# Four attention heads' maxima taken ahead, maxima rows on another queue, keys before queries

## The chip, the core and the metric

One core of one Trainium2 chip runs the whole kernel. The metric is the device time in microseconds (us) of one execution; the median of three runs before the change is 1075.11 us.

## The reference

The input is 2 sequences of 1024 tokens with 128 values each, all f32. Four blocks follow each other, each added to its input and followed by a layer norm:

```python
x = _layernorm(x + _L0_attn_ref(x, ...))   # retention, 8 heads
x = _layernorm(x + _L0_ffn_ref(x, ...))    # causal attention, then experts
x = _layernorm(x + _L1_attn_ref(x, ...))   # full attention
x = _layernorm(x + _L1_ffn_ref(x, ...))    # 128 x 128 matrix, ternary weights
```

The retention has scores `q @ k.T` with a decay by distance and no softmax, then a group norm for each head, a gate (`silu`) and an output matrix. Both attentions have 16 heads of width 8. Each head's row of scores goes through a softmax: exponentials of the scores less the row's maximum, divided by their sum. The first attention is causal; after it each token goes to the one of 4 experts (hidden width 512) that its logits favour. The second attention has biases in queries, keys and values, and two corner scores set to -1e9.

## The kernel before

The work of the two sequences is laid out as two long stages, with TensorE (PE) as the engine that has most to do.

*The retention* runs from the start to about 241 us. It goes through 16 chunks of 128 tokens, one per turn of a loop. A turn n has, in the engines' order: the scores of chunk n; `gated` and `affine` (group norm's scale, bias and gate) of chunk n-1, with VectorE's product `og * sg` (L1018 in the last turn); `weighted` (scores times values, from `sm`), the running state (`carry`, `state`, L858 and L861), `group_norm(n)` (its sum of squares is `ss`, L868, its `rstd` comes from GpSimd, L139 and L140) and `normal` (ScalarE's `on`, L879), and `output(n-1)` with the Wo matrix, residual and the statistics of the layer norm. The PSUM tiles of the stage come from pools of their own; `rwide` gives a tile of two banks. Jobs that make the queries and keys of the first attention for early tokens are placed into turns by a table `plan` and a function `aside`.

*The chain* runs from about 241 us to the end, and covers both attentions. A step (a, b, k, g, h) is attention a, sequence b, key half k of 512 keys (so also which half of the tokens), a group g of 4 heads, and a block h of 256 queries. Each step has three parts, spread over "ticks" of the function `chain_tick`:

- In its s-items, TensorE writes up to 512 scores for each of the 4 heads of the group (`score`, tile `sc`, a bank of PSUM each), and VectorE takes the maxima of each row (`maxima`): L430 with a plain reduction, L425 where the diagonal has to be masked. The result is a column in `parts`.
- After a step's last s-item, `shifts` (L437) joins the parts and negates them (`lowered`). In the next tick `product` has TensorE transpose that (`turn`, L444, into a free corner of the bank `acc`), and `enter` has ScalarE copy it to `m_rows` (L450) and a DMA write it into additional rows of `qT`, from row ONE of each head on (L452, 4 KB, 64 times, on SyncE's queue). These rows are summed into the next scores by the matmul itself, so they come out less the maximum.
- Seven ticks after an s-item (AHEAD = 7), `shifted` has TensorE compute the scores once more, transposed (`sct`: 256 keys by 256 queries of a head in one bank), `exps` has ScalarE take the exponentials of them (L485, tile `es`, four for each tick), `bar` has GpSimd zero the part above the diagonal (L493), and one tick later `product` multiplies by the values into `acc`. ScalarE copies `acc` out (L518 for a first pair of keys, L521 for the others, which GpSimd then adds, L522). Two ticks later `finish` transposes and divides.

One tick of the later kind thus has four `sc`, four `sct` and one `acc`: nine allocations, each the next bank of a ring of the eight PSUM banks (`ring_of`). In chain_tick the heads are taken as (0, 1) and (2, 3): scores of two, shifted scores of two, then the others. The order of the instructions on each engine is written by hand here (`manual_schedule`): an engine takes them strictly in that order. `side_work(tick)` runs before each tick and advances lanes of jobs: generators in which a `yield n` says how many ticks later the next piece may be emitted. There are 208 ticks of items.

Between the two stages stands a stretch written out by hand: ticks 0 to 4 of the chain, among them what the last turn of the retention still has to do: `output(14)`, `normal(15)`, `gated(15)` and `affine(15)` (L907 and L909: og times scale plus bias), the product `og * sg` of chunk 15 (L1044; L1043 ahead of it is an exponential of one value whose result isn't used), `output(15)` (its statistics are L924 to L927), `aside(15, 1)`, and `layer_norm_scalar` (rstd on GpSimd by L139 and L140, shift on GpSimd by L932 and L933, then the norm itself on ScalarE, L935). Ticks 5 and on follow in a loop.

The jobs that the change touches: the experts' lane gathers a sequence's tokens ordered by expert (`e_in`, L1256, a DMA on SyncE), yields 2 ticks (L1257), and transposes them (`xg_ps`, L1265); its weights come by L1236 (`e_w`, SyncE). `attn_inputs` makes values, queries and keys of the second attention for half a sequence; its last loop (L1387) computes `dense` for the queries and then for the keys (ScalarE's bias add, L1393), and `spread` (L280) writes each into `qT` or `kT` with four DMAs on SyncE's queue, one for each head group.

Of the kernel before, what the change touches and what calls it, by code (L numbers as in the profile page):

```python
# [18 lines left out]
NC = BT // P  # L19
QT = 2  # L20
BQ = QT * P
RH, RD, RV = 8, 64, 128
NG, GH, HD = 4, 4, 8
HW = 32
# [40 lines left out]
def block_kernel(  # L65
# [13 lines left out]
    nc = tc.nc  # L79
# [101 lines left out]
    def slot(name):  # L181
        return banks[0](name)
# [213 lines left out]
                if n < len(p):  # L396
                    mm(*p[n])

    def score(item, heads):
        i, pieces = item  # L400
        a, b, k, g, h = steps[i]
        if i not in parts:
            parts[i] = small.tile([P, QT, GH, NB], F32, tag="parts", name="parts")
        got = []
        for j in heads:
            sc = slot("sc")
            rws = hrows(j)
            products = []
            for c, first, n, at, _ in pieces:
                tok = (queries(i) * QT + c) * P  # L410
                products.append((
                    sc[:, at : at + n], qT[b][rws, g, tok : tok + P], kT[b][rws, g, first : first + n]
                ))
            got.append((j, sc, products))
        return got
# [30 lines left out]
    def enter(i, tp):  # L446

        a, b, k, g, h = steps[i]
        rows_of = small.tile([GH * QT, P], F32, tag="m_rows", name="m_rows", bufs=2)
        nc.scalar.copy(rows_of, tp[: GH * QT])  # L450
        at = queries(i) * BQ
        nc.sync.dma_start(out=qT[b][ONE::HW, g, at : at + BQ], in_=rows_of)  # L452

    def diagonal_pair(n_item):
        i, pair = t_items[n_item]
# [109 lines left out]
    def starts(a, b, k):  # L565
        return s_first[step_of(a, b, k, 0, 0)]

    def chain_tick(tick):
        si = tick if tick < n_items else None
        ti = tick - AHEAD if 0 <= tick - AHEAD < n_items else None  # L570


        for s_heads, t_heads in (((0, 1), (2, 3)), ((2, 3), (0, 1))):
            got_s = got_t = ()
            for second in (s_heads[0] > 0, s_heads[0] == 0):
                if second and ti is not None:
                    got_t = shifted(ti, t_heads)
                elif not second and si is not None:
                    got_s = score(s_items[si], s_heads)
            together(*(products for *_, products in (*got_s, *got_t)))  # L580
            if si is not None:
                maxima(s_items[si], got_s)
            if ti is not None:
                exps(ti, got_t)
        if ti is not None:
            bar(ti)
        if si is not None and s_last[s_items[si][0]] == si:
            shifts(s_items[si][0])
        si, entering = tick - 1, None
        if 0 <= si < n_items and s_last[s_items[si][0]] == si:  # L590
            entering = s_items[si][0]
        ai = tick - AHEAD - 1
        if 0 <= ai < n_items:
            product(ai, entering)
        elif entering is not None:
            tp = slot("m_ps")[:, :P]
            turn(entering, tp)
            enter(entering, tp)
        ai = tick - AHEAD - 3
        if 0 <= ai < n_items and t_last[t_items[ai][0]] == ai:  # L600
            finish(t_items[ai][0])


    with ExitStack() as rc:
# [233 lines left out]
        def weighted(n, sm):  # L838
            for g in range(RG):
                for a in range(2):  # L840
                    nc.tensor.matmul(  # L841
                        pout[n][:, a, g, :], sm[:, a, g, :], v[n][:, 2 * g + a, :],
                        start=opens(n) and g == 0, stop=True, skip_group_check=True,
                    )
# [95 lines left out]
        def layer_norm(m, r):  # L940
            for c in range(NC):
# [2 lines left out]
                    ALU.subtract, ALU.mult,  # L944
                )


        plan = {
            (3, 1): (pad, 1), (4, 0): (pad, 1), (4, 1): (pad, 1), (5, 0): (pad, 3),
# [15 lines left out]
        with tc.manual_schedule():  # L965
            for n in range(3):
                transpose_x(n)
            pr = rotary(0)
            center()
            cosines(0, pr)  # L970
            cosines(1, rotary(1))
            values(0)
            gate(0)
            sines(0)
            rotated(0)
            late_loads = load_late()
            next(late_loads)
            block = None
            for n in range(n_chunks - 1):
                before = n > 0  # L980
                keeps = not opens(n + 1)
                sm = scores(n)
                if keeps:
                    kd = keys_by_token(n)
                sines(n + 1)
                rotated(n + 1)
                if before:
                    pt, og = gated(n - 1)
                    affine(n - 1, pt, og, range(RH))
                weighted(n, sm)  # L990
                if keeps:
                    carry(n, kd)
                if before:
                    nc.vector.tensor_tensor(og, og, sg[n - 1], ALU.mult)  # L994
                r = group_norm(n)
                if n + 2 < n_chunks:
                    cosines(n + 2, rotary(n + 2))
                next(late_loads, None)
                gate(n + 1)
                if block:  # L1000
                    layer_norm(*block)
                    block = None
                aside(n, 0)
                normal(n, r)
                if before:
                    block = output(n - 1, og)
                values(n + 1)
                aside(n, 1)
                if n + 3 < n_chunks:
                    transpose_x(n + 3)  # L1010
                if n == 2:
                    dense_weights()
            n = n_chunks - 1
            sm = scores(n)
            pt, og = gated(n - 1)
            affine(n - 1, pt, og, range(RG), range(RG, RH))
            weighted(n, sm)
            nc.vector.tensor_tensor(og, og, sg[n - 1], ALU.mult)  # L1018
            r = group_norm(n)
            aside(n, 0)  # L1020
# [7 lines left out]
        ))  # L1028
        banks[0] = ring_of(ring)
        with tc.manual_schedule():  # L1030
            chain_tick(0)
            output(n - 1, og)
            normal(n, r)
            rs.close()
            ring.append(ctx.enter_context(tc.tile_pool(
                name="ring2", bufs=1, space=PSUM, side="right", reuse_waits="tile"
            )))
            chain_tick(1)
            pt, og = gated(n)
            affine(n, pt, og, range(RH))  # L1040

            unused = small.tile([P, 1], F32, tag="unused", name="unused")
            nc.scalar.activation(unused, col("one"), AF.Exp)  # L1043
            nc.vector.tensor_tensor(og, og, sg[n], ALU.mult)  # L1044
            chain_tick(2)
            chain_tick(3)
            block = output(n, og)
            chain_tick(4)
            alone.clear()
            aside(n, 1)  # L1050
            layer_norm_scalar(*block)
# [161 lines left out]
    def experts(oh, endings_of, quick=False):  # L1213
# [40 lines left out]
        bias_1 = found["bias_1"]  # L1254
        rows_in = scratch("e_rows", "e_in", (P, NT, P))
        nc.sync.dma_start(out=rows_in[:, :n_tiles], in_=by_e)  # L1256
        yield 2  # L1257
        xgT = scratch("e_cols", "xgT", (P, NT, P))
        for at in range(0, n_tiles, NC):
            if at and n > NC:  # L1260
# [102 lines left out]
    def attn_inputs(b, k):  # L1363

        at, name = ((0, "k_first"), (T - 1, "k_last"))[k]
        t = kT[b][:, :, at]
        nc.gpsimd.tensor_tensor(t, t, col(name).to_broadcast([P, NG]), ALU.add)
        if k == 0:

            for g in range(NG):  # L1370
                nc.sync.dma_start(
                    out=qT[b][ONE::HW, g, :],
                    in_=causal[:GH, :P].unsqueeze(1).to_broadcast([GH, T // P, P]),
                )
        tp = transposed(x2[b][k], "x2_ps")
        x2T = scratch("joT", "x2T", (P, BT))
        nc.scalar.copy(x2T, tp)
        yield 1
        pv = by_tile(x2T, lw["wv"], "lpv")
        for c in range(NC):  # L1380
            nc.vector.tensor_tensor(
                v_heads(b)[:, k * NC + c, :, :HD],
                pv[:, c * P : (c + 1) * P].rearrange("p (h d) -> p h d", d=HD),
                row("bv").rearrange("p (h d) -> p h d", d=HD),
                ALU.add,
            )
        for dst, w, name, tag in (  # L1387
            (qT[b], lw["wq"], "bq", "sq"), (kT[b], lw["wk"], "bk", "xn")
        ):
            pr = slot("lpr")  # L1390
            mm(pr, w, x2T)
            dense = scratch(tag, "dense", (P, BT))
            nc.scalar.activation(dense, pr, AF.Identity, bias=bias[name])  # L1393
            spread(dst, k, dense)
        yield 1
# [116 lines left out]
                    lane.pop(0)  # L1512

    with tc.manual_schedule():
        for tick in range(5, last_tick):
            side_work(tick)
            chain_tick(tick)
        side_work(last_tick)
# [132 lines left out]
```

## Time and profile before

| what | before |
|---|---|
| median of 3 runs | 1075.11 us (1066.61 to 1077.7) |
| the profiled execution | 1074.85 us |
| its span, first to last instruction | 1073.2 us |
| mean granted TensorE clock | 0.972 |
| the retention | 0 to about 241 us |
| from the retention to the tick with the first product | about 241 to 283 us |
| exponentials L485 on ScalarE | 418.4 us, 832 of 587 ns |
| maxima L430 on VectorE | 397.6 us, 640 of 682 ns |
| maxima L425 on VectorE | 125.6 us, 256 of 491 ns |
| matmuls `sc`, `sct`, `acc` on TensorE | 423.1, 409.4 and 220.4 us |
| DMA issues of `qT<-m_rows` (L452) | 64 of 4.0 KB, on SyncE's queue |

All but the first two lines of the table come from one execution, recorded by the profiler. PE is TensorE's matmuls, PEld its weight loads (which overlap the matmuls), DVE is VectorE, ACT ScalarE, POOL GpSimd, SP SyncE; SPq is SyncE's queue of DMA issues. In a group's row `out<-in` are the names of the tiles, `xcount` is the number of instructions, and after the bar stand busy time, mean duration in ns, and the idle time of the engine just before these instructions with what ended most of it. In the strip of 40 slices each digit is the busy share in tenths, and a slice is 26.8 us; PEclk is the clock that TensorE was granted, in tenths of its full speed. A row of an engine's order of time has start and duration in us, then engine, line and operation; square brackets hold the idle time before it and what ended that.

### The profile page before, as it was taken

Reading aid. Unit: us, or ns where it says so; the run is one execution under the profiler, and the core shown is the slowest. Engines: PE = TensorE matmul, PEld = TensorE weight load, DVE = VectorE, ACT = ScalarE, POOL = GpSimd, SP = SyncE. Lnnn points to the kernel's source line nnn. Section 1 sums busy time; section 2 is a strip of 40 time slices with the busy share of each in tenths; the row PEclk is TensorE's granted clock in tenths of the full one; section 3 lists DMA queues with packets and bytes.
Section 4 is the critical chain, followed back from the end, with each engine's and each line's share of the span. In section 5 each row is a group of like instructions: output and inputs, shape, how many; then the busy total and the mean of one; then the engine's idle time right before and its main releaser. Section 6 shows DMA issues by size and latency. Waiting matters only on the chain.

```text
span 1073.2 us, 28623 instructions
## 1 busy us (share of the span) xinstructions
PE 1012.6 (94%) x11455; PEld 721.6 (67%) x11455; DVE 768.7 (72%) x1747; ACT 685.8 (64%) x1482; POOL 458.4 (43%) x626
## 2 busy tenths in 40 slices
PE   6999999997899999989999999999999999999995
PEld 5888888875565657765776666677756666666662
DVE  4667686667774867777677787766686888888861
ACT  2555544544575767665767677766676777777774
POOL 2466554533354664465444334425271222222222
PEclk9999999998897999999999999999999999999997
DMA  6522122110100032103311000323102000000000
GB/s 207 141 63 50 40 49 48 24 31 2 39 2 17 6 82 87 39 14 84 93 38 23 3 2 7 102 61 100 29 24 41 2 13 2 13 2 3 11 3 10
DMA packets 31061, 43.10 MB, mean 40 GB/s; under 512 B 4496, under 2 KB 18000, under 8 KB 30800
## 3 DMA queue, kind: packets, MB, share of 16 engines
q1 hardware_dynamic: 29664, 38.89, 14.0%
q0 software_dynamic: 1024, 2.10, 0.7%
q8 instruction: 90, 1.47, 0.6%
q10 hardware_dynamic: 240, 0.29, 0.1%
q14 instruction: 43, 0.35, 0.1%
HBM read 23.83 MB, written 4.46 MB: 26 GB/s over the span
## 4 chain that ended last, share of the span: by engine, by line
PE 74%; DVE 11%; POOL 5%; DMA 4%; issue 2%; ACT 2%; SPq 1%; POOLq 0%; DVEq 0%; ACTq 0%
PE sc L86 17%; PE acc L86 16%; PE sct L86 14%; DVE spare L425 3%; PE ph L86 2%; PE pmoe L86 2%; PE pout L841 2%; PE py L86 2%; PE pr L86 2%; PE pv L86 2%; DVE parts L430 2%; PE o_ps L211 1%; PE mpr L86 1%; PE pg L86 1%; PE psc L86 1%
## 5 line engine op out<-in xcount | busy, mean ns | idle before, releaser
L485 ACT ACTIVATE es<-sct 128x512 f32<-128x512 f32 (+1 forms) x832 | 418.4, 587 | 171.5 <-PE sct L86 150.1
L430 DVE TENSOR_REDUCE parts<-sc 128x1 f32<-128x512 f32 x640 | 397.6, 682 | 105.1 <-PE sct L86 90.1
L86 PE MATMUL sc<-kT,qT 32*128 32x512 f32 (+3 forms) x1792 | 423.1, 585 | 8.7 <-DVE parts L425 5.0
L86 PE MATMUL sct<-qT,kT 32*128 32x256 f32 (+1 forms) x3328 | 409.4, 389 | 3.9 <-DMA qT<-m_rows 3.9
L86 PEld LDWEIGHTS sct<-qT,kT 32*128 32x128 f32 x3328 | 292.5, 187 | 23.7 <-issue 7.9
L522 POOL TENSOR_TENSOR oT<-oT,part 128x256 f32<-128x256 f32 x144 | 104.6, 727 | 331.9 <-ACT part L521 331.4
L86 PE MATMUL acc<-es,v_aug 128*32 128x256 f32 (+1 forms) x3328 | 220.4, 382 | 10.5 <-DVE parts L430 4.2
L86 PEld LDWEIGHTS sc<-kT,qT 32*128 32x128 f32 x1792 | 154.6, 189 | 78.8 <-issue 25.9
L86 PEld LDWEIGHTS acc<-es,v_aug 128*32 128x32 f32 x3328 | 89.7, 111 | 105.8 <-DVE parts L430 40.5
L425 DVE CUSTOM_DVE_ANT_0 spare<-sc,causal 128x128 f32<-128x128 f32 (+3 forms) x256 | 125.6, 491 | 45.0 <-PE sct L86 11.6
L909 ACT ACTIVATE og<-pt,cols_sb 128x128 f32<-128x128 f32 x124 | 45.0, 467 | 43.3 <-PE pt L896 43.3
L493 POOL TENSOR_SCALAR_AFFINE_SELECT es<-es 128x512 f32<-128x512 f32 x64 | 40.3, 635 | 62.7 <-ACT es L485 60.9
L521 ACT COPY part<-acc 128x256 f32<-128x256 f32 x144 | 56.9, 395 | 7.7 <-PE acc L86 6.1
L140 POOL TENSOR_TENSOR rstd<-rstd,nhalf 128x4 f32<-128x4 f32 (+2 forms) x46 | 55.5, 1208 | 3.7
L778 POOL TENSOR_TENSOR qd<-qk,r_rest 128x512 f32<-128x512 f32 x16 | 20.3, 1271 | 49.1 <-DVE qk L775 46.2
L795 ACT COPY v<-pv 128x1024 f32<-128x1024 f32 x16 | 16.2, 1012 | 38.6 <-PE pv L86 38.6
L772 POOL TENSOR_TENSOR swap<-swap,r_cs 128x1024 f32<-128x1024 f32 x15 | 35.4, 2360 | 10.7 <-DMA swap<-plain 10.7
L86 PE MATMUL py<-r_wo,og 128*128 128x128 f32 x256 | 33.1, 285 | 2.5 <-DVE og L994 2.5
L86 PEld LDWEIGHTS py<-r_wo,og 128*128 128x128 f32 x256 | 31.3, 200 | 3.7 <-PE pg L86 1.1
L86 PE MATMUL pv<-r_wv,xT 128*128 128x512 f32 x64 | 30.6, 601 | 2.2 <-DVE qk L768 2.0
L841 PE MATMUL pout<-v,sm 128*128 128x128 f32 x256 | 31.5, 277 | 1.2 <-DVE sm L809 1.2
L86 PE MATMUL pg<-xT,r_wg 128*128 128x128 f32 x256 | 31.4, 276 | 1.1 <-ACT v L795 1.1
(236 smaller groups left out, 1262.8 us busy)
## 6 DMA issues: line engine op xcount, KB each, us to landing
e_w<-in_m_w SPq DMA_DIRECT2D x50, 256.0 KB
swap<-plain SPq DMA_DIRECT2D x62, 128.0 KB
qT<-dense SPq DMA_DIRECT2D x32, 64.0 KB
kT<-dense SPq DMA_DIRECT2D x32, 64.0 KB
x<-in_x SPq DMA_DIRECT2D x4, 256.0 KB
mcs<-in_m_const SPq DMA_DIRECT2D x4, 256.0 KB
qT<-m_rows SPq DMA_DIRECT2D x64, 4.0 KB
e_in<-by_expert SPq DMA_DIRECT2D x2, 448.0 KB
```

Of the source, the lines that this page charges most:

```text
L86: nc.tensor.matmul(o, lhsT, rhs, start=start, stop=stop)
L140: nc.gpsimd.tensor_tensor(r, r, nhalf[:, :n], ALU.pow)
L425: nc.vector.tensor_tensor_reduce(out=spare[:, :n], in0=sc[:, at : at + n], in1=causal[:, BT - n :], scale=1.0, scalar=-3.0e38, op0=ALU.add ...
L430: nc.vector.tensor_reduce(part, sc[:, at : at + n], AX.X, ALU.max)
L485: nc.scalar.activation(es[n_item][:, j, :n], sct[:, :n], AF.Exp, scale=scale)
L493: nc.gpsimd.affine_select(out=d, in_=d, pattern=[[0, GH], [1, P]], compare_op=ALU.is_ge, fill=0.0, base=0, channel_multiplier=-1,)
L521: nc.scalar.copy(part, acc[:, :BQ])
L522: nc.gpsimd.tensor_tensor(sum_, sum_, part, ALU.add)
L772: engine.tensor_tensor(swap[n], swap[n], table(n, 1), ALU.mult)
L778: nc.gpsimd.tensor_tensor(qd[n], rq[n], gq, ALU.mult)
L841: nc.tensor.matmul(pout[n][:, a, g, :], sm[:, a, g, :], v[n][:, 2 * g + a, :], start=opens(n) and g == 0, stop=True, skip_group_check=True,)
L909: nc.scalar.activation(to, of, AF.Identity, bias=bias_, scale=weight)
```

## The change

It has four parts, in the words of the diff:

- The score banks and maxima of tick 0 (all four heads) and of the first two heads of tick 1 are emitted inside the last two turns of the retention, with a new function `ahead_of_time`, in a pair of banks of the retention's `rwide` instead of the ring. Tick 0 is the only s-item of its step, so `shifts` follows there, after heads 2 and 3. `taken` holds that half of tick 1 is done, and `chain_tick(1)` only does heads 2 and 3. `chain_tick(0)` is gone, and each of the hand-written ticks moves up a place: the stretch starts at tick 1 and ends with tick 5, so `output(15)` now comes after tick 4 and the loop begins with tick 6.
- The DMA of the maxima's row is issued by ScalarE's queue, behind the copy that makes the row.
- The experts' lane of the second sequence waits three ticks instead of two before the transposes of the gathered tokens.
- In `attn_inputs` the keys come ahead of the queries.

```diff
-    def score(item, heads):
+    def score(item, heads, bank=lambda: slot("sc")):
...
-            sc = slot("sc")
+            sc = bank()
...
-        nc.sync.dma_start(out=qT[b][ONE::HW, g, at : at + BQ], in_=rows_of)
+        nc.scalar.dma_start(out=qT[b][ONE::HW, g, at : at + BQ], in_=rows_of)
...
+    taken = set()
...
-                elif not second and si is not None:
+                elif not second and si is not None and not (si in taken and s_heads[0] == 0):
                     got_s = score(s_items[si], s_heads)
...
+        def ahead_of_time(tick, heads):
+
+            wide = rwide("sc")
+            at = iter(range(2))
+            got = score(
+                s_items[tick], heads, lambda: wide[:, next(at)].rearrange("p g t -> p (g t)")
+            )
+            together(*(products for *_, products in got))
+            maxima(s_items[tick], got)
+            if heads[0]:
+                assert s_last[s_items[tick][0]] == tick
+                shifts(s_items[tick][0])
+            else:
+                taken.add(tick)
...
                 weighted(n, sm)
+                if n + 2 == n_chunks:
+                    ahead_of_time(0, (0, 1))
                 if keeps:
                     carry(n, kd)
...
                 aside(n, 0)
+                if n + 2 == n_chunks:
+                    ahead_of_time(0, (2, 3))
                 normal(n, r)
...
             affine(n - 1, pt, og, range(RG), range(RG, RH))
+            ahead_of_time(1, (0, 1))
             weighted(n, sm)
             nc.vector.tensor_tensor(og, og, sg[n - 1], ALU.mult)
             r = group_norm(n)
...
-            chain_tick(0)
+            chain_tick(1)
             output(n - 1, og)
             normal(n, r)
...
-            chain_tick(1)
+            chain_tick(2)
             pt, og = gated(n)
             affine(n, pt, og, range(RH))
...
             nc.vector.tensor_tensor(og, og, sg[n], ALU.mult)
-            chain_tick(2)
             chain_tick(3)
+            chain_tick(4)
             block = output(n, og)
-            chain_tick(4)
+            chain_tick(5)
             alone.clear()
             aside(n, 1)
             layer_norm_scalar(*block)
...
-        yield 2
+        yield 2 if n == NC else 3
...
         for dst, w, name, tag in (
-            (qT[b], lw["wq"], "bq", "sq"), (kT[b], lw["wk"], "bk", "xn")
+            (kT[b], lw["wk"], "bk", "xn"), (qT[b], lw["wq"], "bq", "sq")
         ):
...
-        for tick in range(5, last_tick):
+        for tick in range(6, last_tick):
             side_work(tick)
             chain_tick(tick)
```

## The prediction

> **What bounds the kernel now.** I read the busy shares first, then TensorE's own waits, then the granted clock in short windows around each wait, and last the engines' orders of time where something is moved. The page's first two views:
>
> ```profile
> PE 1012.6 (94%) x11455; PEld 721.6 (67%) x11455; DVE 768.7 (72%) x1747; ACT 685.8 (64%) x1482; POOL 458.4 (43%) x626
> ...
> PEclk9999999998897999999999999999999999999997
> ```
>
> TensorE is the bound nearly everywhere: in the later ticks one full tick takes 2.95 us without a hole (starts at 686.65, 689.59, 692.53). So a gain must come from holes in TensorE's row, or from slices with a lower clock. TensorE's waits (us in total, times, longest) name four such holes, all on DMAs that the change touches, besides the start:
>
> ```profile
> PE sct L86 <- DMA qT<-m_rows: 3.9, 3, 1.8
> ...
> PE xg_ps L1265 <- DMA e_in<-by_expert: 1.8, 1, 1.8
> ...
> PE sc L86 <- DMA kT<-dense: 1.0, 1, 1.0
> ```
>
> (The first row is three waits: 1.85, 1.17 and 0.88 us, ended at 331.4, 397.1 and 506.7.) What such a hole costs is more than itself. Windows of 4 us; the columns are the busy times of PE, PEld, DVE, ACT, POOL, then the granted clock:
>
> ```profile
> 328.00:332.00 4.00, 2.15 (x17) 1.16 (x17) 2.53 (x10) 1.25 (x2) 1.17 (x3) 1.00 0.15 18
> 332.00:336.00 4.00, 4.00 (x39) 2.09 (x35) 1.29 (x2) 2.59 (x6) 0.04 (x1) 0.65 0.01 2
> 336.00:340.00 4.00, 4.00 (x13) 2.76 (x12) 0.00 (x0) 1.17 (x2) 0.68 (x1) 0.50 0.00 1
> 340.00:344.00 4.00, 4.00 (x20) 2.08 (x23) 0.27 (x1) 1.26 (x3) 1.61 (x1) 0.50 0.00 0
> 344.00:348.00 4.00, 4.00 (x36) 2.13 (x28) 2.31 (x4) 2.45 (x5) 3.01 (x3) 0.64 0.06 20
> ```
>
> The reader is to see a window with a hole (2.15 of 4 busy), then 16 us with TensorE full and its clock down: work at half speed.
>
> **The change part by part.** *The rows on ScalarE's queue.* Why was the row at 331.4 late? Its copy (L450) ran at 322.0; then SyncE's queue:
>
> ```profile
> 324.41 2.87 SPq L280 DMA_DIRECT2D qT<-dense  x4
> 327.38 0.56 SPq L452 DMA_DIRECT2D qT<-m_rows  x1
> ```
>
> The row lay 5.1 us behind a wait for `dense` and the four issues of it; it landed 3.9 us after its issue began. The same stands at 388.6 to 393.48 (four kT issues ahead) and at 498.9 to 501.29 (part of eight). Issued by ScalarE right after the copy, they come 5.1, 4.6 and 2.4 us sooner; landing even as slowly as the worst of the three (5.3 us), at 327.6, 394.2 and 504.2, they precede the moments where TensorE ran dry (329.6, 395.9, 505.9). All three holes go.
>
> Their price: hole plus clock. First: 1.85 + 4 x (0.35 + 0.50 + 0.50 + 0.36) = 8.7 us. Second, windows of 3 us from 397 at 0.67 and 0.76: 1.17 + 3 x (0.33 + 0.24) = 2.9. Third, from 507 at 0.55 and 0.89: 0.88 + 3 x (0.45 + 0.11) = 2.6. Sum 14.1 us.
>
> Here two rules of the Trainium skill speak against this. "DMA: Bandwidth & Descriptors", section "Issuing engines are not separate DMA queues", says that DMAs of all issuers share the same 16 engines, and that another issuer saves only the sequencer's time to start one. By that the rows would land no sooner and the 14.1 would stay. The rows above show that the lost time is not in the transfer: 5.1 us passed before the issue, in SyncE's order. I take the rows. "TensorE: Matmul & The Clock Gate", section "HAM oscillation — how this bites in real kernels", warns only of idle gaps over about 3.4 us; by it holes of 0.9 to 1.9 us cost no clock, and the three are worth 3.9 us, not 14.1. The trace shows a fall after each of these three, and after the two priced below; but holes of 1.48 us (664.1) and 1.11 us (798.3) left it at 1.00. So I take the measured falls, and keep the idle time alone as the other end.
>
> Against that stands ScalarE's issue time. The nearest row is its own two DMAs (L758): 593 and 602 ns, begun 0.03 us after the copy; SyncE's 64 row issues took 521 to 630. I take 0.57 us, 64 times: 36.5 us if nothing covers it. Queued behind are the copy of `acc` (L518, L521), which frees a PSUM bank, then the four exponentials of the next tick; TensorE waits for both through its ring of eight banks, GpSimd for the copies (it idles 331 us on them, and nobody waits for it). The cover, in a later tick with a row:
>
> ```profile
> 924.20 0.25 ACT L450 COPY m_rows<-acc 8x128 f32<-8x128 f32 x1
> 924.36 0.36 ACT L518 COPY oT<-acc 128x256 f32<-128x256 f32 x1
> ...
> 925.39 2.06 ACT L485 ACTIVATE es<-sct 128x512 f32<-128x512 f32 x4 [0.68 <-PE sct L86]
> ```
>
> ScalarE then idles 0.68 us: the issue fits with 0.1 to spare, and the bank is free at 925.3, before TensorE's fourth pair at 925.47. So the last 32 steps cost nothing. In the first 32 rows come every one to four ticks and the ticks are shorter; I put 0.1 us on each, 3.2 us, an estimate between 0 and the 18.2 of all 32 uncovered. SyncE is rid of 64 waits; expert weights behind them come sooner, but TensorE waits for none of those.
>
> *Keys ahead of queries (L1387).* At 582.02 the queries' four issues went first (2.90 us), the keys at 585.04, landing at about 590.1, and TensorE stood 1.03 us until 590.16; the clock was then 0.77 and 0.66 in 3 us windows. Keys first land 3 us sooner, before 589.1. The queries of that half are first read 30 ticks later. Gain 1.03 + 3 x (0.23 + 0.34) = 2.7 us.
>
> *`yield 3` (L1257).* `e_in`, issued at 691.07, landed 6.3 us later, 1.77 us after its transposes were due; the clock was 0.80 and 0.77 in the next 4 us windows. One tick (2.95) later it has landed with 1.2 to spare: 1.77 + 4 x (0.20 + 0.23) = 3.5 us. What follows slides a tick, keys of the second sequence too, with five ticks (15 us) in hand: no cost.
>
> *Maxima taken ahead.* Tick 0's eight pairs run from 243.71 to 247.31, 3.6 us of VectorE, 1.8 for two heads; two of 512 take 1.7 (steps of 0.84). 5.3 us leave a stretch that VectorE paces: that is the ceiling. In turn 14 VectorE idles 2.44 us before `state` (for L858) and 2.04 before `on` (for rstd). The first 1.8 starts only after `weighted` (226.64) and its 0.64 us of matmuls, so it ends at 229.1 and delays state, og, ss by 0.6; the second hides. In turn 15 the pair stands between L907 and L1018 with no idle: 1.7 more. So `ss` ends 2.3 us later (246.1), and `on` on ScalarE at 250.2 instead of 248.0. Counting on from 246.1 with the same durations (half tick 1 1.7, output 0.85, tick 2 2.85, about 1.2 waiting for `on`, then waiting for og until 255.3, og 1.2, tick 3 3.6) VectorE finishes tick 3 at 260.1, not 261.85. But the last `output` now follows tick 4 (3.4 us) and ends at 264.3 instead of 262.8. A chain hangs on it:
>
> ```profile
> 262.88 0.20 POOL L139 TENSOR_SCALAR rstd<-mv 128x4 f32<-128x4 f32 x1 [15.94 <-DVE mv L927]
> ...
> 272.01 0.24 POOL L933 TENSOR_SCALAR shift<-shift 128x4 f32<-128x4 f32 x1
> ```
>
> Then L935 on ScalarE (272.28, 1.65 us) stands ahead of the first exponentials. Unchanged in length, it releases them at 275.5 instead of 273.98. VectorE's lead is thus stopped there. Before, these exponentials waited 1.48 us between their halves; now they run through and end at 277.2 as before, and tick 8 starts 0.5 to 0.8 us sooner. I take 0.7 gained, between 1.5 lost (that wait stays) and 5.3 gained (the chain is not the brake). The three row issues that stand there lie in ScalarE's idle time.
>
> Sum: 14.1 + 2.7 + 3.5 + 0.7 - 3.2 = 17.8 us. The profiled execution took 1074.85 us (span 1073.2); 1074.85 - 17.8 = 1057.0. The median of the runs, 1075.11, is 0.3 above that execution, so I predict 1057 us.
>
> **The rivals.** (a) *The clock does not pay.* Holes go, but falls of the clock come elsewhere: two longer holes caused none, so which hole does is partly chance. Only idle time counts: 3.9 + 1.0 + 1.8 + 0.7 - 3.2 = 4.2, 1070.7 us. For it: 8.5 of the 20.3 us come from four windows after a single hole. Against it: five of five DMA holes were followed by a fall.
> (b) *The rows land no sooner*, the change doing nothing for them as the first rule says: 1074.85 - 2.7 - 3.5 - 0.7 + 3.2 = 1071.1. Against it: the 5.1 us.
> (c) *ScalarE becomes the brake.* Each issue is paid in full on the way from `acc` to the next exponentials: 36.5 us lost against 21.0 gained, 1090.3 us, slower. It decides from 37 of the 64 issues (21.0 / 0.57). For it: the margin at 924 is 0.1 us, and a row issue may also have to wait on ScalarE for an expert weight load to land (the row after 397.1, with six loads from 395.87). Against it: ScalarE waits for TensorE before exponentials nearly every tick (150.1 us over 193 times).
> (d) *The start gains its ceiling*: 1057.0 - 4.6 = 1052.4, if L935 does not hold the exponentials. It only widens the main case.
>
> **How the numbers follow.** Main case with (d) 0.60, (a) 0.20, (b) 0.10, (c) 0.10. A measurement of this kernel tells about 1% from no change. Under 1064.4 lies the main case: faster 0.60. (a), (b): within 1%, 0.30. (c): slower, 0.10. The range runs from the ceiling with no ScalarE cost (1052.4 - 3.2 = 1049) to just past (b), 1072, leaving out (c). The likeliest case alone: 1049 to 1064.
>
> **What would show it.** TensorE's waits have no row for `qT<-m_rows`, `kT<-dense`, `e_in`; the clock is 1.00 where 332 to 348 stood; the row issues stand on ScalarE's queue with about 0.57 us and its idle time before L485 falls by some 30 us; in the start, `ss` of turn 15 ends about 2.3 us later, and L935 still comes just ahead of the first exponentials. Wrong would prove me: clock falls in new places with no DMA behind them; new TensorE waits on `es`, `part` or `oT`; exponentials starting well before 275.

## The result and the profile after

The changed kernel takes 1079.71 us (median of 8 runs, 1079.11 to 1080.56) against 1073.1 us for the kernel before (8 runs, 1066.61 to 1077.7). The ratio is 1.0058, with a 95% interval from 1.0035 to 1.0081: some 6 us slower, where 16 to 18 us less were predicted. It lies outside the predicted range (1049 to 1072).

The profiled execution took 1079.37 us, its span is 1077.7 us, and its mean granted clock is 0.982 (before: 0.972). So the clock is better and the time is worse. The execution profiled before was a slow one of its kernel, by its clock, so the changed kernel is compared below with profiles at 0.982 and 0.984 too. The page's shares of busy time and the strip of the granted clock:

```profile
PE 1027.4 (95%) x11455; PEld 725.9 (67%) x11455; DVE 768.3 (71%) x1747; ACT 693.1 (64%) x1482; POOL 459.5 (43%) x626
...
PEclk9999999997899999999999999999999999999997
```

TensorE has the same 11455 matmuls and 14.8 us more busy time, at a higher clock. The three holes of the prediction (on rows, on keys, on `e_in`) are gone: TensorE's list of waits names no DMA in the chain any more. The same five windows that ran at half clock before:

```profile
328.00:332.00 4.00, 4.00 (x52) 2.74 (x45) 3.46 (x15) 3.17 (x8) 2.20 (x4) 1.00 0.18 23
332.00:336.00 4.00, 4.00 (x32) 2.32 (x32) 1.26 (x3) 3.06 (x8) 0.72 (x1) 1.00 0.00 1
336.00:340.00 4.00, 4.00 (x49) 2.88 (x48) 2.49 (x4) 2.92 (x6) 3.05 (x2) 1.00 0.01 4
340.00:344.00 4.00, 4.00 (x54) 2.61 (x53) 2.98 (x8) 2.33 (x5) 1.78 (x3) 1.00 0.21 49
344.00:348.00 4.00, 3.30 (x44) 2.04 (x48) 3.53 (x13) 2.14 (x6) 3.63 (x5) 1.00 0.14 17
```

That much went as written. One fall of the clock came in a new place, though: 3.4 us at half clock from 478.9 on, behind 1.6 us of waiting for VectorE's `parts` and no DMA (TensorE's waits from 470 to 480 us, and a window):

```profile
PE acc L86 <- DVE parts L430: 1.6, 1, 1.6
...
478.00:482.00 4.00, 4.00 (x36) 2.93 (x28) 3.74 (x10) 1.46 (x3) 3.92 (x6) 0.62 0.02 4
```

The loss shows in the page's groups, in the idle time just before ScalarE's two copies out of `acc` (the last part of each row; before, L521 had 7.7 us of it and L518 3.8):

```profile
L521 ACT COPY part<-acc 128x256 f32<-128x256 f32 x144 | 56.1, 389 | 21.5 <-ACT m_rows L450 9.7
...
L518 ACT COPY oT<-acc 128x256 f32<-128x256 f32 x64 | 24.3, 379 | 27.7 <-ACT m_rows L450 22.5
```

Together 32.2 us behind `m_rows` L450: that is where ScalarE issues the DMA, and issuing isn't counted as busy. The wait list of TensorE hardly has it:

```profile
PE sc L86 <- DVE r L1444: 1.1, 1, 1.1
...
PE sc L86 <- ACT part L521: 0.7, 1, 0.7
...
PE sc L86 <- ACT oT L518: 0.7, 1, 0.7
```

So the ticks have to be compared one by one. A tick is taken here from the first `acc` matmul of the tick before it to its own. The price of a row shows plainly in the second attention. Some ticks from both profiles (us):

```
tick  row?   before  after
164           3.73    3.15
165   yes     4.08    3.98
166           2.94    4.08     (a job slid by one tick)
167           2.94    2.94
168           3.16    3.16
169   yes     2.94    3.49
173   yes     2.93    3.50
177   yes     2.93    3.50
181   yes     2.94    3.49
```

By tick 126 the changed kernel is 9.1 us ahead, at the end it is 5 us behind. Clock makes up most of the lead: between 300 and 1040 us the execution profiled before ran 27.3 us at half clock, the changed one 3.4. Here is tick 173 in the changed kernel, in order of time (start, duration, engine); before, the same tick is the fence at 924.20 in the prediction:

```profile
925.18 0.26 ACT L450 COPY m_rows<-acc 8x128 f32<-8x128 f32 x1
925.47 0.54 ACTq L452 DMA_DIRECT2D qT<-m_rows  x1
925.58 0.59 PE L86 MATMUL sc<-kT,qT 32*128 32x512 f32 x2
...
926.03 1.14 PE L86 MATMUL sc<-kT,qT 32*128 32x512 f32 x3
926.05 0.37 ACT L518 COPY oT<-acc 128x256 f32<-128x256 f32 x1 [0.61 <-ACT m_rows L450]
...
926.32 1.09 ACT L485 ACTIVATE es<-sct 128x512 f32<-128x512 f32 x2
926.48 0.18 PEld L86 LDWEIGHTS sc<-kT,qT 32*128 32x128 f32 x1 [0.26 <-ACT oT L518]
...
926.49 0.70 PE L86 MATMUL sct<-qT,kT 32*128 32x256 f32 x4
```

The copy of `acc` starts 0.87 us after L450 starts; before, it followed by 0.16 (924.20 and 924.36). The difference of 0.71 is more than the issue itself (0.54): the issue began at 925.47, just after the copy of the row had ended (925.44), while two copies overlap. The bank of `acc` is free at 926.43 and not at about 925.7. And who needs it? A tick makes nine allocations in a ring of eight: `acc` is the last of one tick, so the eighth after it, the score tile of head 3 in the next tick, takes its bank. TensorE works heads 2 and 3 side by side. Before, the scores of both began together, as the third pair:

```profile
925.04 0.59 PE L86 MATMUL sc<-kT,qT 32*128 32x512 f32 x2
```

In the changed kernel head 2 begins alone at 926.03 (the row of three holds its two matmuls and head 3's first), and head 3 follows at 926.48, 0.05 us after the bank is free: its weight load is the row that waits for `oT` L518. What shared the array now runs one after the other, and the tick is 0.56 us longer. Since head 2's matmul runs meanwhile, TensorE counts as busy. That fits the added busy time, and the list of waits, which shows only two events of 0.7 us.

### The profile page after: what moved, and what is told of

It is laid out like the page before. It is cut to its first block, busy times and chain, and to the rows that moved or that the text cites. A ratio compares the mean times of both kernels' runs of the same rounds, so it can differ in the third digit from the quotient of the medians.

```text
span 1077.7 us, 28517 instructions
## 1 busy us (share of the span) xinstructions
PE 1027.4 (95%) x11455; PEld 725.9 (67%) x11455; DVE 768.3 (71%) x1747; ACT 693.1 (64%) x1482; POOL 459.5 (43%) x626
## 3 DMA queue, kind: packets, MB, share of 16 engines
q1 hardware_dynamic: 28896, 38.62, 13.7%
## 4 chain that ended last, share of the span: by engine, by line
PE 75%; DVE 10%; POOL 6%; DMA 3%; ACT 2%; issue 2%; SPq 0%; ACTq 0%; POOLq 0%; DVEq 0%
PE sc L86 19%; PE acc L86 17%; PE sct L86 15%; DVE spare L425 3%; PE ph L86 2%; PE pmoe L86 2%; PE pout L844 2%; PE pr L86 2%; PE o_ps L211 2%; PE py L86 2%; PE pv L86 1%; PE acc L444 1%; PE psc L86 1%; POOL rstd L140 1%; PE pg L86 1%
## 5 line engine op out<-in xcount | busy, mean ns | idle before, releaser
L485 ACT ACTIVATE es<-sct 128x512 f32<-128x512 f32 (+1 forms) x832 | 422.9, 585 | 139.2 <-PE sct L86 124.3
L86 PE MATMUL sc<-kT,qT 32*128 32x512 f32 (+3 forms) x1792 | 445.4, 582 | 12.2 <-DVE parts L425 5.7
L86 PE MATMUL sct<-qT,kT 32*128 32x256 f32 (+1 forms) x3328 | 418.7, 387 | 0.0
L86 PEld LDWEIGHTS sct<-qT,kT 32*128 32x128 f32 x3328 | 286.8, 185 | 19.6 <-issue 1.8
L86 PEld LDWEIGHTS sc<-kT,qT 32*128 32x128 f32 x1792 | 163.6, 188 | 97.2 <-issue 20.6
L86 PE MATMUL acc<-es,v_aug 128*32 128x256 f32 (+1 forms) x3328 | 217.6, 378 | 10.9 <-DVE parts L430 4.9
L521 ACT COPY part<-acc 128x256 f32<-128x256 f32 x144 | 56.1, 389 | 21.5 <-ACT m_rows L450 9.7
L518 ACT COPY oT<-acc 128x256 f32<-128x256 f32 x64 | 24.3, 379 | 27.7 <-ACT m_rows L450 22.5
```

What stands on the lines that cost most here:

```text
L86: nc.tensor.matmul(o, lhsT, rhs, start=start, stop=stop)
L485: nc.scalar.activation(es[n_item][:, j, :n], sct[:, :n], AF.Exp, scale=scale)
L518: nc.scalar.copy(sum_, acc[:, :BQ])
L521: nc.scalar.copy(part, acc[:, :BQ])
```

## The experiments

The theory from these two profiles was this: the row's issue delays the copy of `acc` and with it the bank that the last score tile needs ("the bank"). Its rivals: the issue loads ScalarE wherever it stands ("the load"), or the loss comes from another part. The ratios below are to the kernel before on the same chip.

**The issue after the copy.** The changed kernel with the DMA issued behind the copy of `acc`:

```diff
-        nc.scalar.dma_start(out=qT[b][ONE::HW, g, at : at + BQ], in_=rows_of)
+        return lambda: nc.scalar.dma_start(out=qT[b][ONE::HW, g, at : at + BQ], in_=rows_of)
...
-            enter(entering, acc[:, BQ : BQ + P])
+            issue = enter(entering, acc[:, BQ : BQ + P])
...
             nc.gpsimd.tensor_tensor(sum_, sum_, part, ALU.add)
+        if entering is not None:
+            issue()
...
-            enter(entering, tp)
+            enter(entering, tp)()
```

> The changed kernel, with one edit: ScalarE issues the row's DMA after the copy of acc, no longer ahead of it; everything else stays. Theory (the bank): the issue costs time only because the copy of acc waits behind it, so the bank of acc is free 0.7 us later and the third pair of score matmuls of the next tick waits for it; in the ticks that compare cleanly this was 0.56 us a row, some 24 us in all. Then nearly all of it goes: 1079.7 - 24 = about 1056 us, later ticks with a row 2.95 us instead of 3.50. Rival (the load): 0.55 us of issue on ScalarE delays the four exponentials wherever it stands; then 1077 to 1080 us, and ticks with a row stay at 3.5 us. Rival (the other parts): the loss is not from the rows at all; also about 1079 us.

Measured: 1061.98 us, ratio 0.9905 (0.9876 to 0.9934). By ratio that is 16.4 us less than the changed kernel (1.0058 - 0.9905 = 0.0153, times 1073), for moving one instruction behind another. Of the 31 ticks with a row in the second attention, 22 shrink by 0.55 to 0.57 us, to 2.94; four shrink by 0.3 or 0.7, and five, which are long with other work, don't change. Tick 173 in this kernel has the copy of `acc` 0.16 us behind L450 again, and the third pair together:

```profile
910.55 0.26 ACT L450 COPY m_rows<-acc 8x128 f32<-8x128 f32 x1
910.71 0.36 ACT L518 COPY oT<-acc 128x256 f32<-128x256 f32 x1
910.83 0.54 ACTq L452 DMA_DIRECT2D qT<-m_rows  x1
...
911.39 0.59 PE L86 MATMUL sc<-kT,qT 32*128 32x512 f32 x2
```

TensorE's busy time falls from 1027.4 to 1006.6 us for the same matmuls (the fall of the clock at 478.9, which is gone too, explains only some 1.7 of it). The load as the main cause is out: ScalarE issues the same 64 DMAs. The size was over-expected (24).

**The rows back on SyncE's queue.** The changed kernel without this one part:

```diff
-        nc.scalar.dma_start(out=qT[b][ONE::HW, g, at : at + BQ], in_=rows_of)
+        nc.sync.dma_start(out=qT[b][ONE::HW, g, at : at + BQ], in_=rows_of)
```

> The changed kernel with the rows back on SyncE's queue: only maxima ahead, keys first and three ticks instead of two are left of the change. Theory: 1.6 us gained at the start, 2.1 by keys first (4.4 at the hole less 2.3 given back later), 3.3 by the later transposes, nothing else: 1073.1 - 7.0 = 1066 us, with the three waits for rows still there. Rival (the other parts do the harm): 1079 us or more, since the rows would have been the part that gains.

Measured: 1066.44 us, ratio 0.9947 (0.9928 to 0.9965). As the theory has it: the other three parts gain 5.7 us together, and the rows on ScalarE cost 11.9 net. It also says what the three holes are worth: this kernel has them (4.1 us), the one with the late issue doesn't, and they differ by 0.0042, that is 4.5 us, not 14.1 (each interval is some 2 to 3 us to either side, so this difference is a rough one). It is net of what the late issue itself costs: in the two profiles, the ticks with the first two holes (22 and 36) are 6.6 us shorter with the late issue (3.4 of it half clock), and the other ticks 1.2 us longer in all. This kernel's profile has the same mean clock as the changed one's (0.982), and so shows the price of the rows more cleanly than before's: against it the changed kernel is 5.8 us behind by tick 126 and 15.7 at the end.

**The rows alone.** The kernel before with the one line changed to ScalarE's queue.

> The kernel before with one edit, the row's DMA on ScalarE's queue right behind its copy. Theory: the three waits and the low clock behind them go (12.8 us read from the ticks), some 24.5 us of delayed score matmuls come: 1073.1 + 11.7 = 1085 us. The prediction's own account: 1073.1 - 14.1 + 3.2 = 1062 us.

Measured: 1083.21 us, ratio 1.0096 (1.0067 to 1.0125): 10.3 us slower. The theory was near, the prediction's account of this part (10.9 faster) is refuted.

**The maxima alone.** The kernel before with `ahead_of_time` and the order of the ticks that belongs to it, and nothing else.

> The kernel before with the maxima of tick 0 and half of tick 1 taken ahead, and nothing else of the change. Theory: 1.6 us gained by the first product, and kept: 1071.5 us. The prediction: 0.7 gained, 1072.4. Its ceiling: 5.3 gained, 1067.8. Rival (it harms later): over 1074 us.

Measured: 1074.7 us, ratio 1.0007 (0.9988 to 1.0027): no difference. The 1.6 us of the theory was read from two profiles, and falls when all are laid side by side. The start of the first product (us), in the profiles without and with the maxima ahead:

```
without: before 280.1, rows alone 278.2, keys alone 279.4, three ticks alone 278.5, late issue without maxima 278.7
with:    changed 278.6, maxima alone 277.7, rows on SyncE 277.3, late issue 279.0, swapped buffers 280.5, twice early 278.7, twice late 279.9
```

The means are 279.0 and 278.8, with 2 to 3 us of scatter in each row: nothing is gained at the start either.

**Late issue and swapped buffers.** The changed kernel has one more loss that its rows don't explain: tick 143 takes 6.23 us. VectorE there, in the changed kernel:

```profile
824.02 0.69 DVE L1444 TENSOR_TENSOR r<-lo_ps,x 128x512 f32<-128x512 f32 x1 [2.71 <-DMA qT<-dense]
```

The residual of the second attention's output is written into the buffer "sq", which the queries' `dense` uses; since the queries come last now, their DMA still reads it. The edit to the kernel with the late issue:

```diff
-            (kT[b], lw["wk"], "bk", "xn"), (qT[b], lw["wq"], "bq", "sq")
+            (kT[b], lw["wk"], "bk", "sq"), (qT[b], lw["wq"], "bq", "xn")
```

> The changed kernel with the late issue, and one edit more: the dense tiles of keys and queries swap their buffers (keys in sq, queries in xn), so that the residual r3 of the second attention, which is also written into sq, no longer waits for the queries' DMA. Theory: VectorE's wait of 2.7 us before that residual and the 2.3 us that TensorE loses by it go: 1062 - 2.3 = 1059.7 us. Rival (something else is late in that tick): 1062 us, the tick with that residual stays at about 6.2 us.

Measured: 1055.44 us where before takes 1067.58 on that chip, ratio 0.9901 (0.987 to 0.9932). Tick 143 went from 6.23 to 4.07 us, and VectorE's wait is gone:

```profile
813.31 0.69 DVE L1446 TENSOR_TENSOR r<-lo_ps,x 128x512 f32<-128x512 f32 x1 [0.55 <-ACT part L521]
```

So the wait is real and 2.2 us in the profile, but the time against the late issue alone (0.9905) can't tell the two apart. (The two also come from different sets of runs, see the end.)

**The same without the maxima ahead.** The kernel before, late issue, keys first with the buffers swapped, three ticks.

> The kernel before with the late issue on ScalarE's queue, keys first with the buffers swapped, and three ticks before the transposes, but without the maxima taken ahead. Theory: the maxima ahead gain 1.6 to 2.4 us at the start and about as much is lost later, so it is no slower than the same kernel with them: 1059 to 1062 us. If the start's gain is kept, 1062 to 1064 us.

Measured: 1055.41 us, ratio 0.9908 (0.9875 to 0.9941). The maxima ahead add nothing that can be measured here either; the gain at the start that the expectation speaks of is the scatter shown above. These two kernels beat both the kernel before and the changed one, by about 1.0% and 1.5%.

**Keys first alone.** The tuple's order alone, in the kernel before.

> The kernel before with keys ahead of queries alone. Theory: 1.0 us of hole and some clock behind it gained, 2.3 us lost at the residual that waits for the queries' buffer: 1073.0 - 0.5 to 2.1, so 1071 to 1072.5 us. The prediction had 2.7 gained: 1070.3 us. Rival (it harms): over 1074 us.

Measured: ratio 0.9981 (0.9959 to 1.0002), 2.0 us gained, just not clear of nothing. Its profile has both sides: ticks 82 and 83 are 4.4 us shorter, tick 142 is 1.9 longer (the residual's buffer). The 4.4 are more than hole and clock.

**Three ticks alone.** `yield 2 if n == NC else 3`, in the kernel before.

> The kernel before with three ticks instead of two before the transposes of the second sequence, alone. Theory and prediction agree: 1.8 us of hole and 1.7 of clock: 1073.0 - 3.5 = 1069.5 us. If the fall of the clock doesn't always follow the hole, 1.8 alone: 1071.2 us.

Measured: ratio 0.9972 (0.9951 to 0.9992), 3.0 us gained, between the two figures. Its profile also tells what the hole of the keys costs where the clock stays at full speed, as it does here (1.00 in both windows from 586 to 594 us). The first scores after it, and the same in the kernel with keys first alone, where the hole is gone:

```profile
587.59 1.57 PE L86 MATMUL sc<-kT,qT 32*128 32x512 f32 x3 [1.02 <-DMA kT<-dense]
...
581.07 0.70 PE L86 MATMUL sc<-kT,qT 32*128 32x512 f32 x2
```

Tick 82 takes 5.69 us against 2.90: 2.8 us for 1.02 of idle time. Heads have fallen out of step here too: the first row holds three matmuls in 1.57 us, the second two in 0.70. In the profile of before the half clock adds 1.6 us in ticks 82 and 83. So the 4.4 are 1.0 of hole, 1.6 of clock and some 1.8 in which TensorE is busy, with less side by side. The first hole shows the same at full clock: with keys first alone (clock 1.00 from 328 to 340 us), tick 22 takes 7.12 us with a hole of 1.85, against 4.33 in the changed kernel, which has none there.

The parts by ratio, times 1073: rows +10.3, maxima +0.8, keys -2.0, three ticks -3.0, together +6.1. The whole change measured +6.2. The parts add up; with intervals of 2 to 3 us to either side on each part, that it comes within 0.1 is luck.

**The issue twice.** Each row's DMA cut into two of half the size (two heads each), to see what one more issue costs in either place. Early, as the change has it:

```diff
-        nc.scalar.dma_start(out=qT[b][ONE::HW, g, at : at + BQ], in_=rows_of)
+        for j in range(0, GH, 2):
+            first = ONE + j * HW
+            nc.scalar.dma_start(
+                out=qT[b][first : first + HW + 1 : HW, g, at : at + BQ],
+                in_=rows_of[j * QT : (j + 2) * QT],
+            )
```

> The changed kernel, its row DMA cut into two of half the size (two heads each), both issued by ScalarE where the change put the one: ahead of the copy of acc. Theory (the bank): the copy waits for both, some 0.58 us more a row, and nothing is left to cover it: later ticks with a row take about 4.05 us instead of 3.50, and with some 40 rows that stand in such ticks the time is 23 us over the changed kernel (1.0058 of before), about 1.027 of before. Rival (a fixed cost for any such issue, a semaphore or a queue switch): below 1.012.

Measured: ratio 1.0327 (1.0307 to 1.0348), 29 us over the changed kernel where some 23 were expected. Tick 181, which takes 3.49 us in the changed kernel, takes 4.03. In its order of time the late copy and the late bank stand side by side (two issues of 0.54 us, then the copy, then the weight load that waits for it):

```profile
972.30 1.07 ACTq L454 DMA_DIRECT2D qT<-m_rows  x2
...
973.41 0.37 ACT L523 COPY oT<-acc 128x256 f32<-128x256 f32 x1 [1.14 <-issue]
...
973.84 0.18 PEld L86 LDWEIGHTS sc<-kT,qT 32*128 32x128 f32 x1 [0.79 <-ACT oT L523]
```

Then both behind the copy of `acc`, in the kernel with the late issue.

> The same two half-size DMAs, both issued after the copy of acc, as in the kernel with the late issue (0.9905 of before). Theory (the bank): the same work on ScalarE costs little here, since after the copy it has about 0.68 us idle before the first exponential and the exponentials have slack of their own: later ticks with a row stay at 2.95 to 3.2 us, 0.990 to 0.998 of before. Rival (the load on ScalarE counts wherever it stands): each second issue costs 0.55 us too, about 1.010 of before.

Measured: ratio 1.0042 (1.0024 to 1.0059). The theory had said 0.998 at most, and that was too low: the second late issue costs 0.0137, 15 us. In the second attention's ticks with a row that have no other work for ScalarE, the tick itself keeps its 2.94, and the next is 0.1 to 0.3 us longer; where ScalarE has another job in the tick (157, 165) it costs 0.53. So "the load" is not nothing once two issues stand in a tick: the idle time behind the copy covers about one. A second early issue costs twice as much (0.0269, 29 us).

## Why the prediction was wrong

*Rows sooner on ScalarE's queue: right.* The rows no longer lay behind the `dense` issues, all three holes went, and the clock in 332 to 348 is 1.00. Rival (b) is out.

*Their worth, 14.1 us: wrong, some 4.5, or 6 with the cost of the late issue added.* The step that failed is "Their price: hole plus clock". It took the falls of the clock behind the holes from one execution as if they belonged to the holes. Its own trace spoke against it: the longest hole in the chain, 2.09 us from 472.3 on, was not among those weighed, and the clock stayed at full speed:

```profile
472.00:476.00 4.00, 1.91 (x30) 1.11 (x28) 3.10 (x17) 2.04 (x6) 4.00 (x5) 1.00 0.02 4
476.00:480.00 4.00, 4.00 (x52) 2.89 (x48) 2.48 (x4) 3.15 (x8) 1.49 (x3) 1.00 0.00 0
```

Five kernels keep the first hole, all with 1.83 to 1.85 us of it; the trace's record of the granted clock has half speed behind it for 13.7 us (before), 13.7 (three ticks alone), 3.4 (rows on SyncE), 3.4 (maxima alone) and not at all (keys alone). In rows on SyncE, in windows from just ahead of the hole:

```profile
327.00:331.00 4.00, 2.88 (x20) 2.13 (x20) 0.61 (x2) 1.03 (x2) 0.00 (x0) 0.68 0.00 0
331.00:335.00 4.00, 4.00 (x33) 2.30 (x32) 1.29 (x2) 2.75 (x7) 0.72 (x1) 0.90 0.01 3
335.00:339.00 4.00, 4.00 (x44) 2.11 (x42) 1.78 (x3) 2.81 (x7) 2.17 (x1) 1.00 0.00 0
```

The execution profiled before had a low clock: 0.972, where 43 timed runs of the same kernel had 0.973 to 0.985 (and 1078.6 to 1067.1 us). The rule about idle gaps that the prediction weighed and put aside would have given 3.9 us, nearer than the rows did. It isn't the whole of it: falls of 3.4 us did follow holes of 1.8, and idle time isn't the whole cost of a hole either (2.8 us for 1.85 and for 1.02, at full clock). Rival (a), that which hole is followed by a fall is partly chance, was right, and so was its sign: a fall in a new place (478.9) with no DMA behind it. Its "Only idle time counts" put a hole too low.

*ScalarE's issue, 3.2 us: wrong, about 15 to 16.* (14.8 from the rows alone, 10.3 plus the 4.5 of the holes; 16.4 from the late issue. Both leave out what the late issue itself costs, about 1 us by the ticks above.) This is the step that turned the sign: "the issue fits with 0.1 to spare, and the bank is free at 925.3, before TensorE's fourth pair at 925.47. So the last 32 steps cost nothing." Three things in it were off. The bank goes to head 3, whose scores start in the third pair at 925.04, not in the fourth: the ring's count (nine allocations on eight banks) was there to be read. The issue starts only when the copy of the row has ended, so it delays by 0.71 and not by its own 0.57. And the 0.68 us of idle time on ScalarE stand *behind* the copy of `acc`, while the issue was put ahead of it: they could cover the exponentials, never the bank. The bank, free at 924.71 before, would be free at 925.42, 0.38 after head 3's place. The estimate of 0.1 us for the first 32 had no row at all. Rival (c) had the sign, but not the path: it let each issue delay the next exponentials, and in tick 173 they start 1.14 us after L450 (926.32), against 1.19 before. The path is the other one that the prediction itself named, from the copy of `acc` through the ring to TensorE. Rival (c)'s price was 36.5 us, and its point of decision lay at 37 of the 64 issues, against gains of 21. The real gains were about 9, so 15 us were enough.

*Keys first, 2.7 us: size about right (2.0), in part by luck.* Hole and clock were as counted (1.0 and 1.6 us); some 1.8 more came from heads that no longer fall out of step, and the buffer "sq" took 1.9 back. Neither of the two was foreseen. The prediction looked for readers of the queries, not for the next writer of the buffer that their DMA reads.

*Three ticks, 3.5 us: right (3.0), within an interval of some 2 us to either side.*

*Maxima ahead, 0.7 us: as far as measured, nothing (0.8 lost, from 2.9 lost to 1.3 gained).* The detail was wrong: `ss` of turn 15 starts at 242.2 and not 2.3 us later than the 242.6 of before, so turns 14 and 15 absorbed the added maxima. L938 (L935 before) does stand just ahead of the first exponentials, as written, at 272.46; these started at 274.01, as before, not at 275.5. That this chain is why sooner maxima bring nothing fits, but no run moved it.

With the measured terms the sum would have been 1073.1 - 4.5 - 2.0 - 3.0 + 0.8 + 14.8 = 1079.2 us. (The 14.8 holds the same 4.5, so this is the sum of the parts once more, and no separate proof of either.)

## What to carry to other kernels

An instruction added to an in-order engine is covered only by idle time that lies between it and the first thing behind it that somebody waits for; look for the earliest such reader (here a PSUM bank, found by counting the ring), and put a DMA issue behind it. When an engine is "busy" more for the same instructions, compare stage by stage, since partners that ran side by side may be running one after the other, and no list of waits shows it. Don't price a fall of the clock from a single execution: see whether other runs of the same kernel have it. And don't take the idle time of a hole for its cost: compare the tick with the same tick where the hole is gone.

## What the runs showed of the hardware

One DMA issue on ScalarE took 0.54 us, but 0.71 us of the copy behind it, since it began only when the copy ahead had ended, where two copies started 0.16 us apart. The granted clock went between full and half in pieces of 3.4 us or multiples of it (3.4, 6.8, 10.2, 13.7), and the same hole of 1.85 us was followed by none, one or four of them. In all twelve profiles, every fall between 300 and 1040 us began during a hole of 0.8 us or more in TensorE's row, or within 2.5 us of its end; but the kernel with the late issue has seven holes of 1.1 to 2.0 us there and no fall at all. So in these profiles a fall needs a hole, and a hole need not bring one. In step with the mean clock (the longer runs have the lower one), 43 executions of the kernel before on one chip differ by up to 11 us. One thing stays open: ticks 74, 75 and 131 to 133 take some 3 to 4 us more in all, beyond any row, than in the profile of before, in the changed kernel and in the six kernels of the first and third set of runs, but not in the four of the second set. In tick 74 of two of them (rows on SyncE, maxima alone) ScalarE stands idle for 1.0 us just before L450, which starts 1.3 us after the `acc` that it reads has ended (0.15 in keys alone); the profile doesn't show why. No single edit separates the two groups and the set of runs does, so it may go with the set; that isn't shown. Ratios are to the kernel before in the same set.
